# A feed-forward tile beside attention: transpose and split of the gated channels in a step of their own, one step ahead of their product

## The chip, the core and the metric

The kernel runs on one core of a Trainium2 chip. A core has a matrix engine (PE; its weight loads are shown as PEld), a vector engine (DVE), a scalar engine (ACT), a general engine (POOL, or GpSimd) and an engine that issues transfers (SP). Each engine takes its instructions in the order in which they stand in its queue, and they meet through semaphores. The metric is the device time of one execution in microseconds (us); lower is better.

## What is computed

The input is 4 sequences of 1024 tokens with 256 channels. Four residual layers follow each other, each behind a layer norm: a complex linear recurrence, a sparse feed-forward layer, attention with 8 heads, and the same feed-forward layer again. The change touches the first feed-forward layer:

```python
score_out = softmax(bottleneck(x, so_...))          # 256 logits per token
s_v_out, s_i_out = top_k(score_out, 32)
full = x @ weight
out_branch = full, kept only at s_i_out, times s_v_out
score_in = softmax(bottleneck(x, si_...))
s_v_in, s_i_in = top_k(score_in, 32)
x_sparse = x, kept only at s_i_in, times s_v_in      # the gated channels
in_branch = x_sparse @ weight
return out_branch + in_branch + bias
```

So each token needs two top-32 selections, and its gated channels (`x_sparse`) are multiplied by the 256 x 256 weight.

## The kernel before

Tokens are handled in 32 tiles of 128. The program has four stages: the recurrence with the heads of the first feed-forward layer (f1), then the first 8 tiles of f1 (batch 0), then attention over the four batches, then the second feed-forward layer (f2) over all 32 tiles. The remaining 24 tiles of f1, which belong to batches 1 to 3, run beside the attention of the batch before: while attention works on batch b, the f1 tiles of batch b + 1 are finished.

**Attention.** `Attention.heads` (L856) is the main sequence. One step of it is one head of one tile of 128 queries: four matmuls write 128 x 1024 scores to the PSUM tile `sc` (L886), DVE takes the row maximum `nm` (L890), ACT the exponential `pr` (L894). For every other query tile the probabilities are then turned by a transfer (ACT and POOL split them in two halves, L897 and L898, SP issues the transposing transfer, L899), for the others by PE (`ptp`, L905, copied out by L910). `values_sum` (L920) multiplies them with the values (`pmo`, L930), and transposes the reciprocal of the sums (L938). A batch has 64 steps, all four 256.

**The side work.** Queries, keys, values, output products, heads of f2 and the 24 tiles of f1 are generators. `merge` (L963) runs one step of the main sequence at a time and, after step n, every side generator whose place has come. A side entry has a start place and a distance to its next step, or a list of distances. For a tile of f1 the list is the one in L1213.

**The order within an engine** is not the order in which these generators are run. That order only gives each instruction its priority: the program is built with a scheduler that runs a timeline of its own and gives each engine, at each moment, the ready instruction of the highest priority. Then the order in every queue is fixed.

**PSUM.** In this stage it is held by three tags with two buffers each: `sc` (two banks each), `t` for the transposed probabilities, and `s`. All else takes turns in the two buffers of `s`: `pmo`, the query and key products, the output products `pmy`, and of a tile of f1 the logits `pl`, the transposed channels `px` and the product `pf` (the three tags given to `tile` are "sss").

**A tile of f1** (`Ffn.tile`, L589, with `fine=True`): the logits (L554, L556), their maxima and exponentials; four rounds of MAX8 and MATCH_REPLACE8 on DVE (L674), a step after each; the dense product, which was computed earlier and is loaded from memory (L599), is scaled and gated by DVE (L636). The last step holds all the rest: the scale `sc` of the gated channels on POOL (L656), ACT's normalised channels `xg` (L657), POOL's gating (L658), POOL's addition of the dense branch (L659), and `product`: PE transposes `xg` to `px` (two instructions, L682), the bias goes into `pf` (L685), `split` copies the high part of `px` on ACT (L160) and subtracts it on DVE (L161) into `vt`, six matmuls multiply the parts of `vt` with the parts of the weight (L170, in the order high-high, high-low, low-high for each half of the channels: the first two need only the high part), and DVE adds `pf` to x (L662).

f2 uses the same `tile` and `product`, without parts and without `fine`.

Of the kernel before, what the change touches and what calls it, by code (L numbers as in the profile page):

```python
# [12 lines left out]
F32R = mybir.dt.float32r  # L13
# [8 lines left out]
P = 128  # L22
# [3 lines left out]
KD = D // P  # L26
# [131 lines left out]
def split(nc, hi, lo, src):  # L158

    last = nc.scalar.copy(hi, src).ins  # L160
    nc.vector.tensor_tensor(lo, src, hi.bitcast(F32), ALU.subtract)  # L161
    return last


def products(nc, dst, pairs, start=True, stop=True):


    terms = [(x, y) for a, b in pairs for x, y in ((a[0], b[0]), (a[0], b[1]), (a[1], b[0]))]
    for i, (x, y) in enumerate(terms):
        nc.tensor.matmul(dst, x, y, start=start and i == 0, stop=stop and i == len(terms) - 1)  # L170
# [9 lines left out]
class Banks:  # L180
# [5 lines left out]
    def tile(self, shape, tag, name):  # L186
        return self.pool.tile(shape, F32, tag=tag, name=name, bufs=self.bufs[tag])
# [7 lines left out]
class Lru:  # L195
# [31 lines left out]
    def two(self, name):  # L227
        return [self.cp.tile([P, KD, D], F32R, tag=f"{name}{i}", name=f"{name}{i}") for i in range(2)]
# [259 lines left out]
class Ffn:  # L488
# [100 lines left out]
    def tile(self, i, sp, psum, tags, out=None, fast=False, parts=None, tt=None, fine=False):  # L589


        nc, w = self.nc, self.w
        pool = nc.vector if fast else nc.gpsimd
        x = self.x[i]
        blk, tk = i // 4, slice((i % 4) * P, (i % 4 + 1) * P)
        full = None
        if blk in self.full:
            full = sp.tile([P, D], F32, tag="full", name="full")
            nc.sync.dma_start(full, self.full[blk][:, i % 4, :])  # L599
        pl = psum.tile([P, 2, D], tags[0], "pl")  # L600
        self.logits_product(pl, i)


        nr = TOPK // 8
        m8 = sp.tile([P, 2, nr, 8], F32, tag="m8", name="m8")
        e8 = sp.tile([P, 2, 8], F32, tag="e8", name="e8")
        nm = sp.tile([P, 2], F32, tag="nm", name="nm")
        ssum = sp.tile([P, 2], F32, tag="ssum", name="ssum")
        ex = sp.tile([P, 2, D], F32, tag="ex", name="ex")
        wk = sp.tile([P, 2, D], F32, tag="wk", name="wk")  # L610
        for s in range(2):
            self.ordered(nc.vector.max, m8[:, s, 0, :], pl[:, s, :])
        nc.gpsimd.tensor_scalar(nm, m8[:, :, 0, 0], -1.0, 0.0, ALU.mult, ALU.add)
        for s in range(2):
            nc.scalar.activation(  # L615
                ex[:, s, :], pl[:, s, :], AF.Exp, bias=nm[:, s : s + 1], accum_out=ssum[:, s : s + 1]
            )
            self.last_exp = nc.scalar.activation(e8[:, s, :], m8[:, s, 0, :], AF.Exp, bias=nm[:, s : s + 1]).ins
        yield
        for r in range(nr):  # L620
            for s in range(2 if r else 0):
                self.ordered(nc.vector.max, m8[:, s, r, :], wk[:, s, :])
            for s in range(2):
                v, k = (wk, m8[:, s, r, :]) if r else (ex, e8[:, s, :])
                self.ordered(nc.vector.match_replace, wk[:, s, :], k, v[:, s, :], 0.0)
            if fine and r < nr - 1:
                yield
        pool.tensor_tensor(ex, ex, wk, ALU.subtract)  # L628
        rs = sp.tile([P, 2], F32, tag="rs", name="rs")
        nc.vector.reciprocal(rs, ssum)  # L630
        yield

        q = i % 4
        norm = self.norm[blk]
        if full is not None:
            nc.vector.scalar_tensor_tensor(full, full, rs[:, 0:1], ex[:, 0, :], ALU.mult, ALU.mult)  # L636
            ob = full
        else:
            if tt is not None:
                pf = psum.tile([P, D], tags[2], "pf")  # L640
                self.full_product(pf, tt, q)
            else:
                xn = sp.tile([P, D], F32, tag="fxn", name="fxn")
                with self.tc.issue_after(self.convolved):
                    nc.scalar.activation(
                        xn, x, AF.Identity, bias=norm[:, 1, q : q + 1], scale=norm[:, 0, q : q + 1]
                    )
                pf = self.product(sp, psum, tags, xn, None, parts)
            ob = sp.tile([P, D], F32, tag="ob", name="ob")
            nc.scalar.mul(ob, pf, rs[:, 0:1])  # L650
            pool.tensor_tensor(ob, ob, ex[:, 0, :], ALU.mult)  # L651
        yield

        xg = sp.tile([P, D], F32, tag="xg", name="xg", bufs=2)
        sc = sp.tile([P, 2], F32, tag="sc", name="sc")
        pool.tensor_scalar(sc, norm[:, :, q], rs[:, 1:2], 0.0, ALU.mult, ALU.add)  # L656
        nc.scalar.activation(xg, x, AF.Identity, bias=sc[:, 1:2], scale=sc[:, 0:1])  # L657
        pool.tensor_tensor(xg, xg, ex[:, 1, :], ALU.mult)  # L658
        nc.gpsimd.tensor_tensor(x, x, ob, ALU.add)  # L659
        pi = self.product(sp, psum, tags, xg, w.bias, parts)  # L660
        if out is None or fast:
            nc.vector.tensor_tensor(x, x, pi, ALU.add)  # L662
        else:
            yi = sp.tile([P, D], F32, tag="yi", name="yi")
            nc.scalar.copy(yi, pi)
            nc.gpsimd.tensor_tensor(x, x, yi, ALU.add)
        if out is not None:
            nc.sync.dma_start(out[i // 4][:, i % 4, :], x)
        yield
# [4 lines left out]
            ins = make(*args).ins  # L674
        self.last_topk = ins if self.keep else None

    def product(self, sp, psum, tags, v, bias, parts):

        nc, w = self.nc, self.w
        px = psum.tile([P, KD, P], tags[1], "px")  # L680
        for k in range(KD):
            nc.tensor.transpose(px[:, k, :], v[:, k * P : (k + 1) * P], w.ident)  # L682
        dst = psum.tile([P, D], tags[2], "pf")
        if bias is not None:
            nc.tensor.matmul(dst, w.ones, bias, start=True, stop=False)  # L685
        if parts:
            vt = [sp.tile([P, KD, P], F32R, tag=f"vt{i}", name=f"vt{i}", bufs=1) for i in range(2)]
            split(nc, *vt, px)
            products(
                nc,  # L690
                dst,
                [([t[:, k, :] for t in vt], [t[:, k, :] for t in parts]) for k in range(KD)],
                start=bias is None,
            )
            return dst
        vt = sp.tile([P, KD, P], F32, tag="vt", name="vt", bufs=2)
        nc.scalar.copy(vt, px)  # L697
        for k in range(KD):
            nc.tensor.matmul(  # L699
                dst, vt[:, k, :], w.wf[:, k, :], start=(k == 0 and bias is None), stop=(k == KD - 1)  # L700
            )
        return dst
# [337 lines left out]
def tile_kernel(ctx: ExitStack, tc: tile.TileContext, x_in, w_lru, vecs_in, rows, w_ffn, lin_t, w_attn, w_down, out):  # L1040
    nc = tc.nc
# [20 lines left out]
    w = Weights()  # L1062
# [8 lines left out]
    f1 = Ffn("f1", tc, bp, x, w)  # L1071
# [3 lines left out]
    with ExitStack() as c1:  # L1075
        psum = Banks(c1.enter_context(tc.tile_pool(name="ps1", space=PSUM)), {"pu": 2, "po": 2, "py": 2, "pt": 2})
# [38 lines left out]
        k = NBLK - 1  # L1115
# [14 lines left out]
    with ExitStack() as c2:  # L1130
        sp = c2.enter_context(tc.tile_pool(name="at_s", bufs=2))
# [3 lines left out]
        wfs = two([P, KD, D], "wf")  # L1135
# [3 lines left out]
        with ExitStack() as c4:  # L1139
            psum = Banks(  # L1140
                c4.enter_context(tc.tile_pool(name="ps4", space=PSUM)), {"pl": 2, "px": 1, "pf": 2, "at": 3}
            )
            fp = c4.enter_context(tc.tile_pool(name="f_t", bufs=4))
# [40 lines left out]
        psum = Banks(c2.enter_context(tc.tile_pool(name="ps2", space=PSUM)), {"sc": 2, "t": 2, "s": 2})  # L1184
        at.hp = c2.enter_context(tc.tile_pool(name="at_h", bufs=1))
        fp = c2.enter_context(tc.tile_pool(name="f_s", bufs=2))
        side = []
# [22 lines left out]
        for i in range(TPB, NT):  # L1210
            n = i - TPB
            start = 1 + 6.75 * n if n < TPB else STEPS * (n // TPB) - STEPS + 48.25 + 8 * (n % TPB + 1)
            side.append((start, f1.tile(i, fp, psum, "sss", parts=wfs, fine=True), [1, 1, 1, 1, 1, 2, 1]))  # L1213
        merge(chain(*(at.heads(b, psum) for b in range(B))), side)
        for j in range(2):
            last = at.output(B - 1, 1, psum, range(2 * j, 2 * j + 2), slice(PAIRS - 1, PAIRS), True)
# [1 line left out]
    with ExitStack() as c3:  # L1218
        psum = Banks(c3.enter_context(tc.tile_pool(name="ps3", space=PSUM)), {"pl": 2, "px": 3, "pf": 3})
        fp = c3.enter_context(tc.tile_pool(name="f_e", bufs=4))  # L1220
# [104 lines left out]
```

## Time and profile before

| what | us |
|---|---|
| median of 3 runs (1527.78 to 1530.98) | 1530.5 |
| the profiled execution | 1528.76 |
| its span, first to last instruction | 1527.0 |
| attention, first score matmul to last (376.0 to 1292.0) | 916 |
| of this with tiles of f1 beside it | to about 1070 |
| last feed-forward layer, to the end (from about 1320) | 207 |

Busy time over the whole span is PE 84%, DVE 78%, ACT 67% and POOL 45%. The profile page divides the span in 40 slices and gives the busy tenths of every engine in each. In the lists of waits a line reads: the waiting instruction, what ended its wait, the sum of such waits, how many, the longest. In the timeline a line is: start, duration, engine, source line, operation, written and read tile, and in brackets how long the engine stood idle before it and what ended that.

### The profile page before, as it was taken

Reading aid. Unit: us, or ns where it says so; the run is one execution under the profiler, and the core shown is the slowest. Engines: PE = TensorE matmul, PEld = TensorE weight load, DVE = VectorE, ACT = ScalarE, POOL = GpSimd, SP = SyncE. Lnnn points to the kernel's source line nnn. Section 1 sums busy time; section 2 is a strip of 40 time slices with the busy share of each in tenths; the row PEclk is TensorE's granted clock in tenths of the full one; section 3 lists DMA queues with packets and bytes.
Section 4 is the critical chain, followed back from the end, with each engine's and each line's share of the span. In section 5 each row is a group of like instructions: output and inputs, shape, how many; then the busy total and the mean of one; then the engine's idle time right before and its main releaser. Section 6 shows DMA issues by size and latency. Waiting matters only on the chain. (4 is left out here: it accounts for less than half of the span.)

```text
span 1527.0 us, 28727 instructions
## 1 busy us (share of the span) xinstructions
PE 1286.5 (84%) x10134; PEld 955.6 (63%) x10136; DVE 1184.6 (78%) x3682; ACT 1017.5 (67%) x2152; POOL 680.3 (45%) x849
## 2 busy tenths in 40 slices
PE   4879998697898898888998989889999999566675
PEld 3535465376677766766776767677777777334454
DVE  8976665697868887878768687777676675599998
ACT  5353433566887877797777787877777776475674
POOL 2033332161545454544544554454344444067776
PEclk9999999698999999999999999999999999688899
DMA  3110000321454343434433445334344545000000
GB/s 118 32 41 15 21 21 21 128 97 49 84 93 90 61 77 73 77 70 82 82 74 60 72 79 86 61 61 83 68 82 79 92 86 96 1 15 24 22 25 28
DMA packets 288609, 96.51 MB, mean 63 GB/s; under 512 B 268233, under 2 KB 284626, under 8 KB 288466
## 3 DMA queue, kind: packets, MB, share of 16 engines
q1 hardware_dynamic: 283024, 88.50, 28.7%
q10 hardware_dynamic: 5442, 6.18, 1.2%
q8 instruction: 80, 1.31, 0.4%
q14 instruction: 63, 0.52, 0.1%
HBM read 16.01 MB, written 11.53 MB: 18 GB/s over the span
## 5 line engine op out<-in xcount | busy, mean ns | idle before, releaser
L898 POOL TENSOR_TENSOR pd<-pr,pd 128x1024 f16<-128x1024 f32 x128 | 273.5, 2141 | 247.6 <-ACT pd L897 185.7
L890 DVE TENSOR_REDUCE nm<-sc 128x1 f32<-128x1024 f32 x256 | 308.5, 1217 | 78.9 <-PE sc L886 77.5
L894 ACT ACTIVATE pr<-sc,nm 128x1024 f32<-128x1024 f32 x256 | 285.9, 1119 | 84.6 <-DVE nm L892 47.0
L886 PE MATMUL sc<-kh,qs 128*128 128x512 f32 x512 | 184.3, 438 | 26.4 <-ACT pr L894 18.8
L886 PE MATMUL sc<-kl,qs 128*128 128x512 f32 x512 | 162.0, 397 | 0.0
L674 DVE MATCH_REPLACE8 wk<-m,wk 128x256 f32<-128x256 f32 x384 | 154.9, 406 | 0.1
L910 ACT COPY p<-ptp 128x512 f32<-128x512 f32 x224 | 124.1, 590 | 45.3 <-PE ptp L905 33.7
L674 DVE MAX8 m<-wk 128x8 f32<-128x256 f32 x384 | 151.3, 412 | 0.4
L930 PE MATMUL pmo<-p,la 128*64 128x128 f32 x2048 | 144.0, 289 | 6.1 <-ACT ft L524 2.9
L905 PE MATMUL ptp<-ident,pr 128*128 128x128 f32 x1024 | 138.3, 275 | 12.9 <-ACT pr L894 12.4
L930 PEld LDWEIGHTS pmo<-p,la 128*64 128x64 f32 x2048 | 122.8, 144 | 25.0 <-ACT ft L524 5.1
L905 PEld LDWEIGHTS ptp<-ident,pr 128*128 128x128 f32 x1024 | 115.6, 140 | 34.8 <-ACT pr L894 22.2
L897 ACT CAST pd<-pr 128x1024 f16<-128x1024 f32 x128 | 133.5, 1054 | 5.6 <-DMA d<-pd 4.6
L886 PEld LDWEIGHTS sc<-kh,qs 128*128 128x128 f32 x512 | 85.2, 195 | 51.1 <-ACT pr L894 29.8
L886 PEld LDWEIGHTS sc<-kl,qs 128*128 128x128 f32 x512 | 97.0, 190 | 23.2 <-issue 1.4
L930 PE MATMUL pmo<-d,lb 128*64 128x128 f16 x3072 | 103.4, 222 | 7.6 <-DVE qs L853 2.6
L930 PEld LDWEIGHTS <-lb 128*64 128x64 f16 x3072 | 92.2, 111 | 26.3 <-issue 20.1
L628 POOL TENSOR_TENSOR ex<-ex,wk 128x512 f32<-128x512 f32 x61 | 77.6, 1273 | 57.4 <-DVE wk L674 45.5
L926 POOL COPY rows<-rs 128x128 f32<-128x128 f32 x128 | 36.1, 294 | 124.4 <-PE pmo L938 76.3
L941 DVE TENSOR_TENSOR on<-pmo,rb 128x128 f32<-128x128 f32 x128 | 36.4, 285 | 66.8 <-ACT rb L940 66.3
L147 PE MATMUL pt<-ident,xn 128*128 128x128 f32 x256 | 47.8, 309 | 44.5 <-ACT xn L145 32.9
L699 PE MATMUL pf<-wf,vt 128*128 128x256 f32 x288 | 81.2, 427 | 4.6 <-ACT vt L697 4.2
(307 smaller groups left out, 2768.6 us busy)
## 6 DMA issues: line engine op xcount, KB each, us to landing
tt<-ft SPq DMA_DIRECT2D x16, 256.0 KB
tt<-tt SPq DMA_DIRECT2D x8, 512.0 KB
out<-x SPq DMA_DIRECT2D x32, 128.0 KB
x<-in_x ACTq DMA_DIRECT2D x6, 512.0 KB
pf<-pfs SPq DMA_DIRECT2D x12, 256.0 KB
full<-pf SPq DMA_DIRECT2D x24, 128.0 KB
d<-pd SPq DMA_TRANSPOSE x128
wa<-in_w_attn SPq DMA_DIRECT2D x2, 640.0 KB
```

Of the source, the lines that this page charges most:

```text
L147: nc.tensor.transpose(pt[:, k, i * P : (i + 1) * P], xn[:, k * P : (k + 1) * P], ident)
L628: pool.tensor_tensor(ex, ex, wk, ALU.subtract)
L674: ins = make(*args).ins
L699: nc.tensor.matmul(dst, vt[:, k, :], w.wf[:, k, :], start=(k == 0 and bias is None), stop=(k == KD - 1))
L886: nc.tensor.matmul(sc[:, sl], qs[:, j, q * P : (q + 1) * P], kk[:, sl], start=(i == 0), stop=(i == 1))
L890: nc.vector.tensor_reduce(nm, sc, AX.X, ALU.max, negate=True)
L894: nc.scalar.activation(pr, sc, AF.Exp, bias=nm, accum_out=ssum[:, j : j + 1])
L897: nc.scalar.copy(pd[:, 0, :], pr)
L898: nc.gpsimd.tensor_tensor(pd[:, 1, :], pr, pd[:, 0, :], ALU.subtract)
L905: nc.tensor.transpose(pt[:, kk, :], pr[:, kc * P : (kc + 1) * P], self.ident)
L910: nc.scalar.copy(dst, pt)
L930: nc.tensor.matmul(po[j * HD : (j + 1) * HD, 0, :], v, pts[j][:, c, :], start=(n == 0), stop=(n == len(terms) - 1),)
```

## The change

For the tiles of f1 beside the attention (`fine`), the last step is divided in two. The first of the two holds the scale, `xg`, the gating, the addition of the dense branch, the two transposes to `px` and the split into `vt`; this part from the allocation of `px` on is a new method, `turn`. The second holds the bias, the six matmuls and the addition to x. The list of distances becomes eight ones in place of 1, 1, 1, 1, 1, 2, 1: with s the start place, the old last step stood at s + 7; now the turning stands at s + 6 and the product at s + 7. Number, operands and sizes of all instructions are the same. The other users of `product` get the same instructions in the same program order as before.

```diff
-        pi = self.product(sp, psum, tags, xg, w.bias, parts)
+        vt = None
+        if fine:
+            vt = self.turn(sp, psum, tags, xg)
+            yield
+        pi = self.product(sp, psum, tags, xg, w.bias, parts, vt)
...
-    def product(self, sp, psum, tags, v, bias, parts):
-
-        nc, w = self.nc, self.w
+    def turn(self, sp, psum, tags, v, parts=True):
+
         px = psum.tile([P, KD, P], tags[1], "px")
         for k in range(KD):
-            nc.tensor.transpose(px[:, k, :], v[:, k * P : (k + 1) * P], w.ident)
+            self.nc.tensor.transpose(px[:, k, :], v[:, k * P : (k + 1) * P], self.w.ident)
+        if not parts:
+            return px
+        vt = [sp.tile([P, KD, P], F32R, tag=f"vt{i}", name=f"vt{i}", bufs=1) for i in range(2)]
+        split(self.nc, *vt, px)
+        return vt
+
+    def product(self, sp, psum, tags, v, bias, parts, vt=None):
+
+        nc, w = self.nc, self.w
+        if vt is None:
+            px = self.turn(sp, psum, tags, v, False)
         dst = psum.tile([P, D], tags[2], "pf")
         if bias is not None:
             nc.tensor.matmul(dst, w.ones, bias, start=True, stop=False)
         if parts:
-            vt = [sp.tile([P, KD, P], F32R, tag=f"vt{i}", name=f"vt{i}", bufs=1) for i in range(2)]
-            split(nc, *vt, px)
+            if vt is None:
+                vt = [sp.tile([P, KD, P], F32R, tag=f"vt{i}", name=f"vt{i}", bufs=1) for i in range(2)]
+                split(nc, *vt, px)
...
-            side.append((start, f1.tile(i, fp, psum, "sss", parts=wfs, fine=True), [1, 1, 1, 1, 1, 2, 1]))
+            side.append((start, f1.tile(i, fp, psum, "sss", parts=wfs, fine=True), [1, 1, 1, 1, 1, 1, 1, 1]))
```

## The prediction

> **What bounds the kernel now.** I read the page first (whole-span shares, then the 40 slices), then the busy time by stage, then PE's waits in the attention stage, then the timeline around one tile.
>
> ```profile
> PE 1286.5 (84%) x10134; PEld 955.6 (63%) x10136; DVE 1184.6 (78%) x3682; ACT 1017.5 (67%) x2152; POOL 680.3 (45%) x849
> ...
> PEclk9999999698999999999999999999999999688899
> ```
>
> The 84% is a mean over unlike stages, so I cut the span: the three parts of attention with tiles of f1 beside them, the part without, and the last feed-forward layer. Columns: stretch, length, then busy us (and instructions) of PE, PEld, DVE, ACT, POOL, granted clock, DMA share, GB/s.
>
> ```profile
> 376.00:596.00 220.00, 195.16 (x1878) 152.65 (x1879) 177.65 (x465) 174.02 (x350) 107.59 (x112) 0.98 0.42 78
> 596.00:843.00 247.00, 218.67 (x2144) 173.56 (x2143) 189.51 (x501) 188.73 (x377) 115.48 (x118) 0.97 0.40 75
> 843.00:1090.00 247.00, 219.76 (x2182) 175.93 (x2183) 184.42 (x474) 187.51 (x372) 114.49 (x115) 0.97 0.40 73
> 1090.00:1283.00 193.00, 180.12 (x1959) 145.83 (x1958) 130.24 (x267) 142.79 (x257) 84.78 (x73) 1.00 0.46 83
> 1320.00:1527.00 207.00, 139.66 (x515) 91.46 (x516) 195.13 (x824) 128.81 (x398) 135.95 (x216) 0.85 0.06 21
> ```
>
> Beside the tiles PE is busy 89% (195.16 / 220, 218.67 / 247), without them 93% (180.12 / 193); DVE and ACT stand at 75 to 81%. The last layer is DVE's (195.13 of 207). The change acts in the first three rows, so the question is which of PE's idle time there (633.59 of 714 busy, so 80 us idle) belongs to the gated product. PE's waits in the stretch 376 to 1283, longest first:
>
> ```profile
> PE sc L886 <- ACT pr L894: 18.8, 22, 2.8
> PE ptp L905 <- ACT pr L894: 12.4, 16, 1.8
> PE pt L147 <- DVE qs L853: 9.0, 5, 2.1
> PE sc L886 <- DVE qs L853: 6.7, 7, 1.7
> PE pf L170 <- DVE nm L892: 5.1, 6, 1.3
> ...
> PE pf L170 <- ACT vt L160: 3.7, 9, 0.7
> PE pl L554 <- DVE x L662: 3.4, 2, 1.7
> ```
>
> With 3.0 us for `pf` on DVE's `vt` (4 times), the product's waits are 5.1 + 3.7 + 3.0 = 11.8 us over 24 tiles, 0.8% of the span. The "DVE nm L892" among them is the same wait: the low part L161 stands right behind it, as the timeline of one tile shows (number 8; I count the 24 from 0).
>
> ```profile
> 606.35 0.38 PE L682 MATMUL px<-ident,xg 128*128 128x128 f32 x2
> 606.56 0.27 PE L685 MATMUL pf<-bias,ones 128*128 128x256 bf16 x1
> 606.76 0.37 ACT L160 CAST vt<-px 128x256 fp32r<-128x256 f32 x1 [1.29 <-PE px L682]
> 607.19 0.50 PE L170 MATMUL pf<-wf,vt 128*128 128x256 f32 x2 [0.35 <-ACT vt L160]
> 608.12 0.14 DVE L892 TENSOR_SCALAR nm<-nm 128x1 f32<-128x1 f32 x1
> 608.18 0.41 DVE L161 TENSOR_TENSOR vt<-px,vt 128x256 fp32r<-128x256 f32 x1
> 608.65 0.73 PE L170 MATMUL pf<-wf,vt 128*128 128x256 f32 x4 [0.96 <-DVE nm L892]
> ```
>
> PE turns, then stands 0.35 us for the high part and 0.96 us for the low part, because two row maxima (2.35 us together) are ahead of L161 on DVE.
>
> **The change part by part.** It adds, removes and resizes nothing: two transposes, one ACT copy (0.39 us), one DVE subtraction (0.41 us), seven matmuls and one addition per tile stay. No transfer is issued in a moved step; SP's transposing transfers keep their producers. What moves is priority: scale, `xg`, gating, dense addition, `px` and `vt` rise by one step (a step is (843 - 596) / 64 = 3.9 us), the product keeps its place. So the price is wholly in the order of the queues, and I read that off the two built programs, tile by tile, on PE between `px` and the first product.
>
> *Stalls now*, from the timeline of all 24 tiles: tile 0 1.29; 2 1.69; 5 0.19; 6 0.16; 8 1.31; 11 1.01; 12 1.25; 15 0.68; 16 1.31; 19 1.02; 20 1.23; 23 0.68; the others none. Sum 11.8, as above.
>
> *Order then.* Tiles 8, 11, 15, 16, 19 and 23 still have transposes, bias and product side by side: their 1.31 + 1.01 + 0.68 + 1.31 + 1.02 + 0.68 = 6.0 us stay. Tile 0 gets the next tile's logits in between, which take 1.09 us on PE (426.43 to 427.52 in tile 1's timeline): 1.09 of its 1.29 are covered. Tile 2 gets two value sums (some 4 us): all of its 1.69. Tiles 5 and 6 get many steps' work: 0.35. Tiles 12 and 20 have eight probability transposes moved behind `px`, 0.88 us (726.05 to 726.93): 2 x 0.88 = 1.76. Gain: 1.09 + 1.69 + 0.35 + 1.76 = 4.9 us.
>
> *What it costs.* Tile 7 loses a cover: now a pair of score matmuls stands between its bias (over at 576.38) and its product (578.10), behind a wait of 0.69 us for ACT; then the product comes at once, and must wait for the high part (ready at about 577.75) and the low part (578.22), about 1.4 + 0.2 = 1.6 us in place of 0.69: 0.9 us more, and the score matmuls behind it are late by as much. In tiles 0, 1 and 3 the next tile's `pl` takes the second buffer of `s` while `px` holds the first; in tile 3 a value sum stands next and needs a buffer, so it waits for L161. By tile 8's row (606.35 to 608.59, 2.24 us from `px` to the end of L161, less 1.09 us of `pl`) that is 1.1 us for one tile; below, 0 if DVE comes at once (L160 0.37 + L161 0.41 fit under `pl`). In tile 3 the low part stands directly behind a row maximum in DVE's queue, and that maximum's scores are done before `px`, so I take 0 and keep 1.1. Behind such a wait stand the next scores, and DVE and ACT wait for those.
>
> *Other orders that shift.* The waits of `pl` for L662 (3.4 us, tiles 9 and 17, one each) could shrink, as a pair of scores leaves the way of the product; 0 to 3.4, I take 0, since the buffer is still given up by L662. The last layer's queues on DVE and POOL are also permuted among neighbours though its code is the same: its DVE idles 207.0 - 195.1 = 11.9 us, and a quarter of that either way, 3 us, bounds it; I take 0, having no reason for a sign.
>
> *Sum.* 4.9 - 0.9 = 4.0 us. The profiled execution would go from 1528.76 to 1524.8; it lies 1.7 us under the median, inside the 3.2 us spread of the runs, so against the median 1530.5 - 4.0 = **1526.5 us**.
>
> **A rule that speaks against it.** The Trainium skill, "Perfetto Trace Analysis", section "Identifying the Most-Contended Engine", says that matmul busy time is no good measure, weight loads are, and that the engine with the highest occupancy is the one to improve. By weight loads PE is at 152.65 / 220 = 69% in the first stretch and DVE at 81%: a PE stall would then be slack, the gain 0, the time 1530.5. Against it stands a row of DVE's waits in the same stage: DVE stands 76.4 us waiting for scores from PE before L890, far more than PE waits for DVE in any one row. The pace passes through PE's order, so I take 4.0; the rule keeps a chance of its own below.
>
> **Rivals.**
> - *The gain is taken up elsewhere.* PE gets to the next scores sooner and waits there for ACT's exponential (already 18.8 us, 22 times). For it: DVE and ACT at 75 to 81% with chains between. Against: 93% for PE where no tile runs. Time: 1530 (within 0.2%).
> - *More than counted.* The 3.4 us of `pl` go too and the last layer gains 3: 4.0 + 3.4 + 3 = 10.4, so 1520. For it: `pf` and `px` no longer sit in both buffers of `s` for the whole split. Against: six of twelve stalls are unchanged in order.
> - *Slower: the wait moves to the buffers of `s`.* `px` is taken earlier and held until L161; whatever wants a buffer next (`pl`, `pmo`, the query products) stands in PE's queue in the product's place, with the whole attention behind it. The Trainium skill, "PSUM — Partial Sum Buffer", section "PSUM bank collisions raise a hardware error", has a bank closed to a second engine even at other columns; so no user can share `px`'s bank before L161 is over, 2.24 us in tile 8's row. If the columns could be shared this would cost nothing; by the rule it costs 1.1 us a place. It decides from four places on (4 x 1.1 against 4.0). At ten of the 24 tiles it is 11 - 4 = 7 us slower: 1537.5. For it: `s` has two buffers for ten kinds of tiles. Against: only tiles 0, 1 and 3 show `pl` directly behind `px`.
> - *The change does nothing*: excluded as a whole, since the queues differ (in the first batch's attention throughout), but from step 64 on most tiles keep their order, which is part of the "taken up" case.
>
> **How the numbers follow.** Forecast 1526.5 (0.2 to 0.5% faster): 0.34. More than counted, 1520: 0.08. Taken up or nothing, 1530: 0.24. Slower by the buffers, 1537: 0.25. Slower by the reshuffled queues alone (the last layer's 3 us and new stalls in the first batch): 0.09. About 0.2%, 3 us, is what a measurement of this kernel can tell from no change. So faster 0.42, same 0.24, slower 0.34. The forecast's own range is 1523 to 1528. The whole range reaches from 1518 (1520 less 1.5 of spread) to 1540 (1537.5 and the last layer's 3).
>
> **What would show it.** Right: PE's waits before the product `pf` (L170) fall from 11.8 to about 7 us, with tiles 0, 2, 12 and 20 free of them and 8, 11, 15, 16, 19, 23 as now; the first stretch (376 to 596) shorter by some 2 us, the next two by 1 each; the last layer 207 us. Wrong: PE waits of `pmo`, `pl` or the query products on L161 or L160 that are not there now; a longer first stretch; or PE's wait for `pr` grown from 31.2 us (18.8 + 12.4) by what `pf` lost.

## The result, and the profile after

The changed kernel takes 1538.09 us (median of 6 runs, 1532.99 to 1541.09) against 1527.9 us of the kernel before on the same chip (6 runs, 1525.05 to 1530.98): a ratio of 1.0063 [1.0047, 1.0079], so 10.2 us or 0.6% slower. The forecast was 1526.5. Its profiled execution took 1540.70 us (span 1539.0), which is 12.0 us more of span than before.

In the changed kernel the source lines of attention and of the addition to x lie further down: scores are L901, row maximum L905 (turned into `nm` by L907), exponential L909, turned probabilities L920, value sums L945, transposition to `px` L685, bias L699, addition `pf` to x L666, query copies L867 and L868. The split (L160, L161) and the products (L170) keep their numbers. The page's whole-span shares and clock row:

```profile
PE 1293.5 (84%) x10136; PEld 961.9 (63%) x10136; DVE 1188.7 (77%) x3682; ACT 1015.0 (66%) x2152; POOL 680.1 (44%) x849
...
PEclk9999999699999999999999999999999999678988
```

The work is the same in kind and number; PE is busy 7.0 us longer with it (1293.5 against 1286.5). The stretches of the prediction had fixed bounds in time; to compare two executions I cut at the same piece of work instead: from the first exponential of attention step 0, 64, 128, 192 to the next of these, so that a row is one batch. Columns as before: stretch, length, then busy us (and instructions) of PE, PEld, DVE, ACT, POOL, granted clock, DMA share, GB/s. Before the change:

```profile
380.70:608.30 227.60, 201.71 (x1989) 158.07 (x1988) 183.17 (x476) 180.32 (x364) 114.85 (x120) 0.99 0.44 80
608.30:855.20 246.90, 218.59 (x2140) 173.77 (x2140) 188.52 (x497) 187.83 (x375) 114.50 (x116) 0.97 0.39 74
855.20:1098.20 243.00, 216.83 (x2185) 173.24 (x2187) 182.19 (x471) 185.44 (x367) 111.27 (x111) 0.97 0.40 73
1098.20:1294.30 196.10, 182.90 (x1939) 148.31 (x1936) 133.93 (x273) 148.51 (x265) 89.14 (x74) 1.00 0.47 86
```

After it, with the last feed-forward layer as the fifth row:

```profile
382.30:616.70 234.40, 205.47 (x1989) 161.98 (x1988) 187.55 (x476) 180.72 (x365) 115.03 (x120) 0.96 0.44 78
616.70:865.60 248.90, 219.23 (x2140) 175.03 (x2140) 188.64 (x497) 187.28 (x375) 114.36 (x116) 0.96 0.39 73
865.60:1108.10 242.50, 215.94 (x2185) 173.47 (x2187) 182.37 (x471) 184.33 (x367) 111.13 (x111) 0.97 0.40 73
1108.10:1305.90 197.80, 184.51 (x1939) 149.51 (x1936) 133.88 (x273) 148.58 (x265) 89.12 (x74) 0.99 0.48 86
1332.00:1539.00 207.00, 139.46 (x516) 91.10 (x514) 194.56 (x824) 127.36 (x397) 135.69 (x216) 0.82 0.06 21
```

The first batch is 6.8 us longer (234.4 against 227.6), the three others +2.0, -0.5 and +1.7, the time ahead of attention +1.6; the last layer takes 207.0 in both. In the first batch PE is busy 3.8 us longer with the same 1989 instructions, at a granted clock of 0.96 in place of 0.99, and idle 3.0 us longer (28.9 against 25.9). A second trace with the same queues in this batch, shown with the first experiment, has it 3.9 us longer; so 3.9 to 6.8 us is as close as the traces place it.

Now the waits that the change was to shorten. PE's waits over the whole attention after the change, some of its rows, longest first; columns: what waits, what ended the wait, us in total, how many, the longest:

```profile
PE sc L901 <- ACT pr L909: 18.8, 15, 3.0
PE ptp L920 <- ACT pr L909: 17.4, 16, 1.8
PE sc L901 <- DVE qs L868: 9.6, 7, 2.6
...
PE pmo L945 <- DVE x L974: 3.6, 3, 1.3
PE pmo L945 <- ACT ex L615: 3.4, 7, 0.9
PE pmy L170 <- DVE on L956: 3.2, 1, 3.2
...
PE pf L170 <- ACT vt L160: 2.8, 7, 0.7
...
PE pf L170 <- DVE vt L161: 2.7, 4, 0.7
...
PE pf L170 <- DVE nm L907: 1.9, 2, 1.0
```

The three rows of `pf` sum to 7.4 us, from 11.8. But `ptp` waits 17.4 for the exponential (12.4 before), scores 9.6 for the queries (6.7), and `pmo` now waits for the exponentials L615 of the logits, which hold a buffer of `s`. All waits of PE in the attention sum to 92.9 us before (376 to 1292) and 97.9 us after (376 to 1306): what `pf` lost, others gained, and 5.0 us on top of it.

One place in the first batch shows how. It lies at attention steps 55 to 57, in the timeline of PE, ACT and DVE; columns: start, duration, engine, line, operation, tiles, count, and in brackets the idle time before and what ended it. Before the change:

```profile
562.74 0.75 PE L170 MATMUL pf<-wf,vt 128*128 128x256 f32 x4 [0.16 <-DVE vt L161]
...
563.33 1.54 PE L170 MATMUL pmq<-xnt,wqk 128*128 128x512 f32 x6
...
565.79 0.60 ACT L852 CAST qs<-pmq 64x512 fp32r<-64x512 f32 x1
...
567.94 0.74 PE L886 MATMUL sc<-kh,qs 128*128 128x512 f32 x2 [0.21 <-DVE qs L853]
```

After it:

```profile
560.43 0.39 PE L554 MATMUL pl<-linb,ones 128*128 128x512 bf16 x1
...
563.35 0.96 PE L170 MATMUL pf<-wf,vt 128*128 128x256 f32 x6
...
564.15 0.73 PE L901 MATMUL sc<-kh,qs 128*128 128x512 f32 x2
...
565.11 0.48 ACT L615 ACTIVATE ex<-pl,nm 128x256 f32<-128x256 f32 x1
...
565.18 1.53 PE L170 MATMUL pmq<-xnt,wqk 128*128 128x512 f32 x6
...
566.21 1.15 ACT L909 ACTIVATE pr<-sc,nm 128x1024 f32<-128x1024 f32 x1
...
567.31 1.07 ACT L912 CAST pd<-pr 128x1024 f16<-128x1024 f32 x1
...
568.25 1.15 ACT L909 ACTIVATE pr<-sc,nm 128x1024 f32<-128x1024 f32 x1
...
569.35 0.58 ACT L867 CAST qs<-pmq 64x512 fp32r<-64x512 f32 x1
...
571.15 0.69 DVE L868 TENSOR_TENSOR qs<-pmq,qs 64x512 fp32r<-64x512 f32 x1
...
571.90 1.16 PE L901 MATMUL sc<-kh,qs 128*128 128x512 f32 x2 [2.59 <-DVE qs L868]
```

`pf` itself is now free of its wait: six matmuls in one run. But the query products `pmq`, which stood right behind it, now come behind a group of scores, and their copy on ACT comes behind two exponentials and a cast: 2.6 us from the end of the product to the copy (566.71 to 569.35), where it was 0.9 (564.87 to 565.79). PE then waits 2.59 us for the queries in place of 0.21, and the pair of score matmuls behind the wait takes 1.16 us in place of 0.74. The change moved no query work; its place in the queues followed from the gated tile's new priorities. Such a loss is in part won back: counted from the first exponential, the changed kernel's steps are 5.9 us behind those of the kernel before at step 26, 0.2 us ahead at step 38, 1.0 behind at step 54, 4.0 at step 58, 3.5 at step 60 and 6.7 at step 64.

### The profile page after: what moved, and what is told of

Its sections match the earlier page's. It is cut to its first block, busy times and chain, and to the rows that moved or that the text cites. A ratio compares the mean times of both kernels' runs of the same rounds, so it can differ in the third digit from the quotient of the medians.

```text
span 1539.0 us, 28719 instructions
## 1 busy us (share of the span) xinstructions
PE 1293.5 (84%) x10136; PEld 961.9 (63%) x10136; DVE 1188.7 (77%) x3682; ACT 1015.0 (66%) x2152; POOL 680.1 (44%) x849
## 5 line engine op out<-in xcount | busy, mean ns | idle before, releaser
L913 POOL TENSOR_TENSOR pd<-pr,pd 128x1024 f16<-128x1024 f32 x128 | 273.6, 2141 | 244.0 <-ACT pd L912 162.1
L905 DVE TENSOR_REDUCE nm<-sc 128x1 f32<-128x1024 f32 x256 | 308.4, 1218 | 76.3 <-PE sc L901 74.2
L909 ACT ACTIVATE pr<-sc,nm 128x1024 f32<-128x1024 f32 x256 | 286.1, 1120 | 98.3 <-DVE nm L907 62.7
L901 PE MATMUL sc<-kh,qs 128*128 128x512 f32 x512 | 186.1, 442 | 29.2 <-ACT pr L909 18.8
L901 PE MATMUL sc<-kl,qs 128*128 128x512 f32 x512 | 163.0, 399 | 0.0
L920 PE MATMUL ptp<-ident,pr 128*128 128x128 f32 x1024 | 141.2, 278 | 17.5 <-ACT pr L909 17.4
L945 PE MATMUL pmo<-p,la 128*64 128x128 f32 x2048 | 143.9, 288 | 9.0 <-DVE qs L868 2.9
L920 PEld LDWEIGHTS ptp<-ident,pr 128*128 128x128 f32 x1024 | 118.2, 142 | 38.0 <-ACT pr L909 25.9
L945 PEld LDWEIGHTS pmo<-p,la 128*64 128x64 f32 x2048 | 122.4, 144 | 30.1 <-issue 6.4
L901 PEld LDWEIGHTS sc<-kh,qs 128*128 128x128 f32 x512 | 87.0, 198 | 54.2 <-ACT pr L909 27.9
L901 PEld LDWEIGHTS sc<-kl,qs 128*128 128x128 f32 x512 | 97.9, 191 | 23.3 <-issue 1.0
L945 PE MATMUL pmo<-d,lb 128*64 128x128 f16 x3072 | 103.1, 222 | 10.9 <-ACT ex L615 3.4
L945 PEld LDWEIGHTS <-lb 128*64 128x64 f16 x3072 | 92.9, 111 | 28.8 <-issue 22.5
L556 PE MATMUL pl<-lint,xc_f 128*128 128x512 f32 x128 | 73.7, 664 | 9.6 <-ACT xc_f L587 9.6
```

Of the source, the lines that this page charges most:

```text
L556: self.last_logits = nc.tensor.matmul(v, x, w.lint, start=False, stop=True).ins
L901: nc.tensor.matmul(sc[:, sl], qs[:, j, q * P : (q + 1) * P], kk[:, sl], start=(i == 0), stop=(i == 1))
L905: nc.vector.tensor_reduce(nm, sc, AX.X, ALU.max, negate=True)
L909: nc.scalar.activation(pr, sc, AF.Exp, bias=nm, accum_out=ssum[:, j : j + 1])
L913: nc.gpsimd.tensor_tensor(pd[:, 1, :], pr, pd[:, 0, :], ALU.subtract)
L920: nc.tensor.transpose(pt[:, kk, :], pr[:, kc * P : (kc + 1) * P], self.ident)
```

## The experiments

Three accounts of the 10 us stood at the start. *Buffers*: `px` is taken earlier, the two buffers of `s` are short, something else waits for them. *Order*: the first batch's queues come out differently as a whole, and by chance worse. *Division*: something in the new step itself, anywhere in the 24 tiles. The ratios below are all against the kernel before, on the same chip, with 95% intervals; its medians there were 1528.9 to 1529.4 us. A ratio can differ by 0.1% from the quotient of the two medians; differences in us are of medians.

**Where: the first batch's tiles alone, and all but these.** The change is kept for one group of tiles only.

```diff
-        if fine:
+        if fine and early:
...
+            early = n < TPB        # the second kernel: n >= TPB
-            side.append((start, f1.tile(i, fp, psum, "sss", parts=wfs, fine=True), [1, 1, 1, 1, 1, 1, 1, 1]))
+            side.append((start, f1.tile(i, fp, psum, "sss", parts=wfs, fine=True, early=early), [1] * 8 if early else [1, 1, 1, 1, 1, 2, 1]))
```

The first eight tiles changed:

> The change for the 8 tiles beside the first batch's attention alone; the other 16 tiles keep the undivided step at s + 7. The built queues are those of the change up to step 64 and nearly those of before behind it, the last layer's too. Theory A (the loss sits in the first batch's reordered queues: the traces show attention's first batch 6.5 us longer, the second 2.0, the third 0.6): 7 to 8 us slower than before. Theory B (every tile pays alike): 8 of 24 tiles, so 3 us slower. Theory C (the permuted last layer pays): no change.

The other sixteen changed:

> The change for the 16 tiles beside the second and third batch alone; queues up to step 64 are exactly those of before, behind it those of the change, and the last layer's order is permuted too. Theory A: 2 to 3 us slower. Theory B: 7 us slower. Theory C: all of it, 10 us slower. If the stalls in front of the product were all that counts (it lost 3.9 us of them in these two batches), it would be up to 3 us faster.

Measured: 1538.48 us, 1.0054 [1.0034, 1.0073], for the first eight; 1529.3 us, 0.9996 [0.9984, 1.0008], for the other sixteen. The whole loss comes with the edit of the first batch's eight tiles. In the second kernel the queues are those of before up to step 64, and from there on those of a changed program: the division in batches 2 and 3 and the permuted queues of the last layer cost nothing and bring nothing. *Division* as such is out for these sixteen tiles.

The two kernels also give a scale, since the second has the first-batch queues of the kernel before and the first has those of the changed kernel. The first took 231.5 us for the batch (234.4 in the changed kernel), the second 228.7 us (227.6 before); one row each, columns as above:

```profile
383.90:615.40 231.50, 203.53 (x1989) 160.50 (x1987) 186.98 (x476) 180.80 (x365) 115.02 (x120) 0.97 0.45 79
379.50:608.20 228.70, 204.11 (x1989) 160.67 (x1988) 182.53 (x476) 180.56 (x365) 114.83 (x120) 0.98 0.44 80
```

Step by step, from one exponential to the same one in the other trace, each pair agrees within 0.3 us up to step 50: with the queues fixed, the pace is fixed. The 2.8 us that part the changed kernel from the first one arise after step 50 at two places, where only the changed kernel's trace has the PE clock at half (last section). So a difference of up to some 3 us between two profiled batches means nothing by itself. It also means that the first batch shows only 3.9 to 6.8 us of the 10; in the first kernel's trace 3.2 us more lie ahead of attention and 3.0 in the third batch, which its edit does not touch. This rest is not explained.

**What: `px` out of `s`, with the change and without.** The three letters name the PSUM tags of `pl`, `px` and `pf`; `t` is the tag of the turned probabilities.

```diff
-            side.append((start, f1.tile(i, fp, psum, "sss", ...
+            side.append((start, f1.tile(i, fp, psum, "sts", ...
```

With the change:

> The whole change, with the transposed channels px in the two PSUM buffers of the probability transposes in place of the shared s buffers. If the loss is the earlier and longer hold of an s buffer by px (the rival of the prediction), this gives it back: about the time of before or a few us less, with PE's waits of pmo and pmy in attention back to 10 us. If the buffers are not the cause, it stays 5 us or more slower, or moves the wait to the probability transposes.

Without it:

> The kernel before with px in the buffers of the probability transposes, and nothing else: the fourth corner beside before, the change, and the change with px there (11.8 us faster than before). If px in the s buffers is what makes the early turning dear, the two kernels with px outside differ little or the changed one is the faster: this one 1517 to 1525. If px outside s is a gain of its own and the early turning costs the same 8 to 10 us as before, this one is at about 1508.

Measured: 1517.47 us, 0.9911 [0.989, 0.9931], with the change, and 1528.31 us, 0.9992 [0.9979, 1.0005], without. With `px` in the buffers of the turned probabilities the change is 10.8 us faster than the kernel it is put into. That looks like *buffers*, but the size behind that account is wrong: in the first batch `px` (from its first transposition to the end of L161) holds its buffer for a mean of 3.05 us before and 2.05 us after the change, so it sits shorter, not longer. Moving a tag also gives all queues another order, so these two runs alone can't part the two accounts. The forecast for the second, 1517 to 1525 or about 1508, missed: its third batch is 5.1 us shorter than before (237.9 against 243.0), and its first 4.9 longer (232.5 against 227.6).

**The whole step one earlier, and the divided step one later.** The first has no division; the list is cut so that turning and product both come one step earlier.

```diff
-            side.append((start, ..., [1, 1, 1, 1, 1, 2, 1]))
+            side.append((start, ..., [1, 1, 1, 1, 1, 1, 1]))
```

> No division: the old undivided last step, but one step earlier (distances of 1 throughout). Its queues from step 64 to 256 are nearly those of the change; up to step 64 they differ from both. If dividing the step is what costs (the first batch's logits and sums come between px and the product), it is within 3 us of before plus the later batches' 2 to 3 us. If placing the gated channels earlier is what costs, it is as slow as the change, 8 to 11 us.

The second is divided, with the turning at the old place and the product a step later. It computes something else: the last tile's product then comes at place 56.25, behind the layer norm by which attention reads that tile (place 56), so there the gated branch is missing from what attention reads; the amount of work is the same.

```diff
-            side.append((start, ..., [1, 1, 1, 1, 1, 1, 1, 1]))
+            side.append((start, ..., [1, 1, 1, 1, 1, 2, 1, 1]))
```

> The step divided, but the turning left at its old place s + 7 and the product put one step later, at s + 8. If the loss comes from the gated channels being placed earlier (the undivided early step was 14 us slower), this is within 3 us of before. If it comes from the division, which lets other users of the s buffers in between px and the product, this is as slow as the change, 8 to 11 us, since the gap between the two is as wide.

Measured: 1545.14 us, 1.0091 [1.0069, 1.0112], and 1537.65 us, 1.005 [1.0032, 1.0067]. Earlier without division loses 16 us, later with division loses 8. Three different edits of the step (the change too) all lose, in both directions of time, so no rule of "early" or "late" explains it. By its own forecast the second run, 8 us slower, would speak for the division. Its trace, of an execution that was 5.6 us under that median (1532.06), does not: its first batch is shorter than before (223.8 us against 227.6), and the second and third, whose tiles it moves too, are 248.7 and 247.5 us (246.9 and 243.0 before). In the first run's trace the first batch is the long one, 238.2 us. So the two lose at different places as far as the traces show it, which fits *order* better than one cause in the step. The first batch of the second run:

```profile
379.30:603.10 223.80, 203.60 (x2034) 160.08 (x2033) 182.86 (x476) 179.73 (x365) 114.52 (x120) 0.98 0.47 82
```

**Queries two steps earlier**, in the changed kernel, for the first batch: does the late query copy of the timeline above account for the loss?

```diff
-                (n + nb * 32 + 8 * g - 7, at.queries(b, nb, g, psum, "s"), 1)
+                (n + nb * 32 + 8 * g - (7 if b else 9), at.queries(b, nb, g, psum, "s"), 1)
```

> The whole change, with the query products of the first batch given their priority two steps earlier. In the changed kernel the score matmuls of step 57 wait 2.6 us for queries whose product came after px, pl and pf in the s buffers. If late queries are how the loss is paid, this gives back 3 us or more of the 10; if not, it stays within 2 us of the change.

Measured: 1534.34 us, 1.0024 [1.0014, 1.0034]. It is 4.9 us slower than the kernel before on its chip (3.7 by the ratio), where the change was 10.2, so it gives back 5 to 6 of the 10 us. Since it too permutes the queues, and its first batch is only 2.5 us shorter than the changed kernel's (231.9 against 234.4), this agrees with the late queries as a part of the loss; it doesn't show that they are that part.

**The test of *order*: the same code at other places.** If the loss is the order's and not the change's, then moving the first eight tiles by half a step, in the kernel before, must cost as much.

```diff
-            start = 1 + 6.75 * n if n < TPB else ...
+            start = 1.5 + 6.75 * n if n < TPB else ...   # also 0.5 and 0
```

The kernel before, at 1.5 and at 0.5:

> The kernel before, with all first-batch tiles started half a step later (1.5 + 6.75 n): the same code, a permuted queue up to step 64, the later batches as before. Theory R (any permutation of the first batch's queues moves it by several us, and before happens to stand well): 4 to 10 us slower than before. Theory P (the early turning in the shared buffers is what costs): within 2 us of before.

> The kernel before, with all first-batch tiles started half a step earlier (0.5 + 6.75 n). Theory R: 4 to 10 us slower than before, or by chance as much faster. Theory P: within 2 us of before, or 1 to 3 us slower, since the whole tile comes earlier.

The changed kernel, at 1.5 and at 0.5:

> The changed kernel, with all first-batch tiles started half a step later: half of the turnings are back at the step they had before. Theory R: anywhere from 8 us faster to 8 us slower than the change. Theory P: about half of the loss is given back, 4 to 6 us slower than before.

> The changed kernel, with all first-batch tiles started half a step earlier. Theory R: anywhere from 8 us faster to 8 us slower than the change. Theory P: the turning is earlier still, 10 to 14 us slower than before.

Both at 0:

> The kernel before with all first-batch tiles started one step earlier (6.75 n). If its own place is an exception, 5 to 16 us slower than before, as at the two half steps; if the half steps are the exception, within 3 us.

> The changed kernel at the same place. If the change has its forecast gain of some 4 us away from that one place, 2 to 8 us faster than e16; if there is no gain of its own, the difference has either sign.

| first start, in steps | without the change | with it | difference, us |
|---|---|---|---|
| 0 | 1540.01, 1.0064 [1.0041, 1.0086] | 1526.84, 0.9984 [0.9975, 0.9993] | -13.2 |
| 0.5 | 1537.71, 1.0056 [1.0034, 1.0079] | 1534.74, 1.004 [1.0024, 1.0056] | -3.0 |
| 1 | 1527.9, 1 | 1538.09, 1.0063 [1.0047, 1.0079] | +10.2 |
| 1.5 | 1545.34, 1.0098 [1.0077, 1.0119] | 1538.61, 1.0067 [1.005, 1.0084] | -6.7 |

These are the runs that decide. Half a step more or less, about 2 us of place and not one instruction changed, makes the old kernel 8.8 to 16.4 us slower, where "the early turning is what costs" had allowed 2 or 3; at three of four places the changed kernel is the faster of the two, though at 0.5 the two intervals overlap. The place 1 is the best of the four for the old code and, with 1.5, the worst for the new. The rows of the first batch show the same thing in the trace: without the change at 1.5 and at 0, and with the change at 0 (one row each, columns as above).

```profile
381.30:620.20 238.90, 208.59 (x1989) 163.45 (x1988) 183.69 (x476) 180.83 (x365) 114.65 (x120) 0.96 0.44 76
```

```profile
382.10:619.10 237.00, 207.17 (x1991) 163.06 (x1989) 183.79 (x474) 180.66 (x365) 114.67 (x120) 0.96 0.45 77
```

```profile
378.90:602.40 223.50, 203.06 (x1990) 161.94 (x1989) 180.57 (x474) 179.71 (x365) 114.26 (x120) 0.97 0.48 82
```

Against the 227.6 us before at its own place, the first two spend 11.3 and 9.4 us more in this one batch, of spans that are 16.6 and 13.2 us longer (1543.6 and 1540.2 against 1527.0); the third is shorter by 4.1 in a span of 1522.7. The busy time of DVE, ACT and POOL differs by 3 us at most from that before; what moves most in the first two rows is PE: 6.9 and 5.5 us more of busy time, which goes with a lower clock (0.96 for 0.99), and 4.4 and 3.9 us more of idle time.

**Which buffer matters: `pl` out of `s`.** Of the gated tile's three users of `s`, the logits hold longest: in the first batch 5.3 us on average before and 5.4 with the change, from the first matmul of `pl` to the end of the second exponential L615 (in the timeline of the changed kernel above 5.16, from 560.43 to 565.59, the end of the exponential that starts at 565.11), against 2 to 3 us for `px`.

```diff
-            side.append((start, f1.tile(i, fp, psum, "sss", ...
+            side.append((start, f1.tile(i, fp, psum, "tss", ...
```

With the change, and without it:

> The whole change, with the next tile's logits pl, in place of px, in the buffers of the probability transposes. In the changed kernel pl comes between px and the product in six of the first batch's tiles and holds the second s buffer until its exponentials are done. If that pair of holds is the cause, this is at the time of before or faster (1520 to 1530). If px's hold alone is the cause, it stays 5 us or more slower than before; and pl, held longer than px, could block the transposes, slower still.

> The kernel before with the logits pl in the buffers of the probability transposes: the control of the change with the same move (1505.6 us, 23.8 us faster than before). If the buffers give the gain, this is at 1500 to 1510. If the early turning is what can use the free buffer, it is at 1515 or above.

The same two at the place 1.5, without the change and with it:

> As e9, started half a step later in the first batch. With the shared buffers this shift cost the kernel before 16 us. If a freer pair of buffers makes the order matter less, within 4 us of e9; if permuting the queue costs as before, 8 us or more away from it.

> The change with pl outside the shared buffers, started half a step later in the first batch. If the change has a gain of its own there, faster than e14 by about as much as e7 is than e9; if the difference is only the permuted queue, the two pairs differ in sign or by more than 5 us.

And `pl` and `px` both moved, with the change:

> The change with pl and px both in the buffers of the probability transposes, pf alone of a tile's PSUM left in the shared ones. If each relief of the shared buffers counts, faster than with pl alone (1505.6), 1498 to 1503; if the transposes' two buffers then become the crowded ones, slower than that, 1508 to 1520.

| buffers and place | without the change | with it | difference, us |
|---|---|---|---|
| `pl` out of `s`, 1 | 1511.14, 0.9883 [0.9865, 0.9901] | 1505.62, 0.9837 [0.9814, 0.9861] | -5.5 |
| `pl` out of `s`, 1.5 | 1524.65, 0.9958 [0.9941, 0.9976] | 1513.13, 0.9907 [0.9895, 0.992] | -11.5 |
| `px` out of `s`, 1 | 1528.31, 0.9992 [0.9979, 1.0005] | 1517.47, 0.9911 [0.989, 0.9931] | -10.8 |
| `pl` and `px` out, 1 | not run | 1517.37, 0.9922 [0.9901, 0.9942] | |

The version with the change and `pl` in the buffers of the turned probabilities beats both kernels: 1505.62 us, 1.6% under before. Its first three batches:

```profile
381.10:610.20 229.10, 206.56 (x1991) 163.29 (x1991) 184.68 (x476) 181.41 (x365) 114.74 (x120) 0.96 0.47 80
610.20:843.90 233.70, 211.54 (x2144) 169.94 (x2142) 188.17 (x498) 186.65 (x375) 113.93 (x116) 0.99 0.42 78
843.90:1074.70 230.80, 207.74 (x2129) 168.31 (x2129) 181.57 (x468) 186.40 (x367) 110.81 (x111) 0.98 0.43 77
```

And the second batch of the one without the change:

```profile
611.90:846.40 234.50, 213.51 (x2142) 171.63 (x2141) 188.60 (x498) 186.97 (x374) 114.24 (x116) 0.97 0.42 78
```

Here the second and third batch drop from 247 and 243 us to about 234 and 231, in both kernels alike: 11 to 15 us a batch. With the first eight tiles shifted they are as short (234.6 and 234.3 us without the change, 237.8 and 228.5 with it), and with `pl` in `s` no shift of these tiles had brought them under 245 and 242 us. So this is no luck of one order of the first batch; a buffer that was short is the likely cause. In PE's waits of these two batches, `pmo`'s for the logits' exponentials L615 (1.9 us before, 3.4 with the change) and the 3.4 us of `pl` for L662 (before) are gone. That is 5.3 of the 23.4 us that the two batches lose without the change; the rest is PE's busy time (12.1 us less) and other waits. Moving the tag also gives these batches other queues, and they were not shifted with `pl` outside, so what the new order adds is not measured. The first batch, 229.1 and 231.0 us, doesn't share the gain: there the order still rules. At the place 1.5 it takes 241.6 us without the change, and the shift costs 13.5 us in all (1511.14 to 1524.65), nearly the 16.4 us that it cost with `pl` in `s`: the freer buffers did not make the order matter less. Moving `px` as well loses 12 us of this again (1517.37): the three batches take 234.9, 238.3 and 235.2 us. `pl`, `px` and the turned probabilities then share the two buffers of `t`; that these are short now is only argued. The forecasts for `pl` out of `s` missed with the change, by 14 us and more (1520 to 1530), and narrowly without it (1500 to 1510, or 1515 and above); the one for both tags moved held (1508 to 1520).

## Why the prediction was wrong

- *The stalls before the product*: right, tile by tile. 11.8 us became 7.4, where 7 was forecast; tiles 0, 2, 12 and 20 are free of them, and 8, 11, 15, 16, 19 and 23 keep theirs (15 and 23 wait 1.02 us each, from 0.68). Tile 7 waits 0.68 us, where 1.6 was forecast.
- *The last layer*: right at 207 us, and the run with only the later tiles changed shows no cost of its permuted queues.
- *The second and third stretch shorter by 1 us each*: +2.0 and -0.5 in the profiles, 0 by the run with only the later tiles changed (0.9996). Too small to tell.
- *The first stretch shorter by some 2 us*: wrong, and here it is decided: 6.8 us longer in the profile, 3.9 in the second trace with the same queues. The step that failed is "Other orders that shift", which took 0 and bounded what could go astray by 3.4 us for `pl` and 3 us for the last layer. It went through PE's order between `px` and the first product, so it priced the product's neighbours and took the rest of the first batch as unchanged, though the prediction itself notes that its queues differ throughout. Moving the same code by half a step shows what that term can be worth: 8.8 us (at 0.5), 10.8 us (at 0), 16.4 us (at 1.5), each against the old place on the same chip, in place of the 0 that I took. Two of the signs that the prediction named for being wrong appeared: the longer first stretch, and PE's wait for `pr`, which grew from 31.2 to 36.2 us (18.8 + 17.4), by 5.0 where `pf` lost 4.4. The third, new waits on L160 or L161 for a buffer, did not.
- *The gain of 4.0 us*: over the seven pairs that differ by the change alone, it is worth +10.2, -6.7, -3.0, -13.2, -10.8, -5.5 and -11.5 us, a mean of -5.8 with a standard error of 3.0 (their spread, 7.9, over the root of 7). The direction of the forecast holds in six of seven. That mean is under two standard errors from nothing, three of the pairs have other buffers (in two the sides ran on different chips), one is within the noise, and the two pairs with `pl` out differ by 6.0 us, more than the 5 that were set beforehand as the limit for a gain of the change's own. So the 4.0 us is neither confirmed nor refuted; if it is there, an order effect of some 14 us (10.2 + 4.0) of the other sign stood beside it at the one place where the change was made.
- *The rival "Slower: the wait moves to the buffers of `s`"* named 1537 to 1537.5 us, next to what was measured, by a mechanism that the traces don't bear out: on average `px` holds its buffer shorter than before in the first batch, the waits that it named are not there, and taking `px` out of `s` leaves the kernel before at its time. With the change, `px` out of `s` is 20.6 us faster than in it (1517.47 against 1538.09), so a part of that mechanism is not excluded. The rule that a bank is closed to a second engine, on which the rival leaned, is tested by no run here. The rival that was right is "Slower by the reshuffled queues alone", which had 0.09 and was thought of as some 3 us. That the number of another rival came close is luck.
- *The skill's rule of the most-contended engine* would have made the gain 0 with DVE as the bound. Neither it nor my count is what the runs show: in the best version DVE's busy time in the second batch is 188.17 us against 188.52, ACT's 186.65 against 187.83, and the batch is 13.2 us shorter, all of it PE's busy time (211.54 for 218.59) and idle time. What helped was to free a PSUM buffer, and no engine's occupancy names it.

What stays open: which of the many permuted instructions of the first batch cost how much. The late queries may be one of them (2.59 us at one place; moving them gave back 5 to 6 us of 10). Where the loss of the changed kernel lies outside the first batch is open too. And the part of the clock is not settled: 0.96 stands in the slow first batches, but also in the best version's (229.1 us), and 0.97 in one of 223.5 us.

## What to carry to other kernels

Where a scheduler fixes the queues from priorities, a local edit is two edits: what it was meant to do, and a new order for everything near it. Measure the second first, by moving the untouched kernel by half a step, and compare the edit at several places; an effect smaller than that spread is not read off one pair. And ask of each PSUM tag how long its tenants hold it: here the one with the longest hold was the one to move out.

## What the runs showed of the hardware

**The PE clock drops to half in short spells, and not by the length of the wait ahead.** In the changed kernel the granted clock is 1.00 from 545 to 548 us, 0.51 from 548.0 to 551.4 and again 0.51 from 571.9 to 575.3. PE waits 1.08 us for an exponential and 2 us later has a value sum that takes 3.46 us, and 2.59 us for the queries and then has a pair of score matmuls that takes 1.16 us (shown above):

```profile
545.81 0.73 PE L901 MATMUL sc<-kh,qs 128*128 128x512 f32 x2 [1.08 <-ACT pr L909]
...
547.82 3.46 PE L945 MATMUL pmo<-p,la 128*64 128x128 f32 x32
```

The kernel with only the first eight tiles changed runs the same queue, and its trace has the same two waits at the same work:

```profile
547.61 0.73 PE L901 MATMUL sc<-kh,qs 128*128 128x512 f32 x2 [1.09 <-ACT pr L909]
...
549.61 1.97 PE L945 MATMUL pmo<-p,la 128*64 128x128 f32 x32
...
572.17 0.72 PE L901 MATMUL sc<-kh,qs 128*128 128x512 f32 x2 [2.60 <-DVE qs L868]
```

There the clock is 1.00 from 540 to 580 us, the value sum takes 1.97 us and the pair 0.72 us. It is the other way around at the first long wait for an exponential: 2.78 us to 390.25 in this trace, with the clock at 0.50 from 389.8 to 393.2; 2.76 us to 388.74 in the changed kernel's, with the clock at 1.00 from 385 to 400. In the first batches of these two traces, of the kernel before and of the one with the other sixteen tiles changed, all spells of low clock begin inside a PE wait of more than 1 us or at most 2.3 us behind it; but the same wait brings a spell in one trace and none in the other. So no wait here lowers the clock by its length alone. The Trainium skill, "TensorE: Matmul & The Clock Gate", section "HAM oscillation — how this bites in real kernels", gives as its abstract rule that PE should have no idle gaps above about 3.4 us; by it none of these waits, the longest of them 2.78 us, should cost clock, which holds for each of them in one trace and not in the other. What else decides is not shown. Where the steps of the two traces part, after step 50, lie the changed kernel's spells at 548 and 572 us (some 1.5 us each); the spell at 390 us left no such mark. Summed over attention, the clock that was not granted makes 18.8 us before and 29.7 us after (1 less the clock, times 5 us, from 376 to 1306). As the spells differ between traces with the same queues, this is not a measure of the change.

**A short vector instruction can last until an instruction of POOL ends.** One of the layer norm's instructions on four columns, in the kernel before:

```profile
489.75 2.15 POOL L898 TENSOR_TENSOR pd<-pr,pd 128x1024 f16<-128x1024 f32 x1
489.89 2.04 DVE L56 TENSOR_SCALAR ax_rs<-ax_v 128x4 int32<-128x4 int32 x1
...
582.08 0.17 DVE L56 TENSOR_SCALAR ax_rs<-ax_v 128x4 int32<-128x4 int32 x1
```

It takes 0.17 us at one place and 2.04 us at another, where it ends at 491.93, within 0.03 us of POOL's end at 491.90. In the changed kernel L65 takes 1.71 us to 492.58 (POOL's L913 ends at 492.56), and L64 2.04 us to 495.90 (POOL 495.89). So what runs beside such an instruction, and with it the order, can change how long it lasts. It is a small part here: these instructions of the first batch take 9.1 us before, 10.9 with the change and 10.9 in the kernel before at 1.5.
